# Norm statistics by block transposes, and their pieces put first and last in a step

## The chip, the cores and the metric

One core of a Trainium2 chip runs the whole kernel. The metric is the device time of one execution in microseconds (us), the median of three runs: 1723.39 (1720.31 to 1724.66) for the kernel before. TensorE multiplies matrices, VectorE works elementwise, ScalarE evaluates functions such as Sqrt and Silu, GpSimd (POOL) copies one partition's row to all partitions and issues some DMAs, SyncE (SP) issues the other DMAs. SBUF is the on-chip memory with 128 partitions, PSUM the memory that TensorE writes.

## What is computed

Four sequences of 1024 tokens with 1024 features pass four residual stages. Each stage ends in a norm over the features, without weights:

```python
x = L0_attn_data
x = _layernorm(x + _L0_attn_ref(x, ...), axis=-1)   # stage 0: product with a block-masked weight
x = _layernorm(x + _L0_ffn_ref(x, ...), axis=-1)    # stage 1: dense layer with a LoRA
x = _layernorm(x + _L1_attn_ref(x, ...), axis=-1)   # stage 2: a sequence model, below
x = _layernorm(x + _L1_ffn_ref(x, ...), axis=-1)    # stage 3: dense layer, LoRA mixed by a router
```

The sequence model projects to 128 features and runs four layers. Each layer does a norm, Silu, a long convolution (done here as a scan), a second norm and a small MLP with 512 hidden features; behind the last layer comes one more norm, and a projection back to 1024 features. All is float32.

## The kernel before, in words

In stages 0, 1 and 2 the activations lie with features on partitions and tokens along the free axis, in groups of 512 tokens (eight groups, g = 0 to 7; a sequence b is two groups). The big products of stages 0, 1 and 3 are done by seven half-size products in place of eight (Winograd's form of Strassen), so VectorE forms sums of operands ahead (`right_sums`, `left_sums`) and adds each product to its outputs (`z<-mm,z`) behind.

The mean is taken out of the weights beforehand, so a norm needs only the mean of the squares over the features, which are partitions. `rstd_rows` (L233) does this for 512 tokens. Four small products with the constant matrix `avg` (32 columns of 1/D) each take 128 tokens and write 32 equal rows, so that the PSUM tile `ps` of 128x128 holds the four quarters of the tokens in four groups of 32 equal rows. ScalarE takes the root of the whole tile into `sd` (L243), VectorE takes the reciprocal of the whole tile (L244), and `spread` (L247) has GpSimd copy one row out of each group of 32 to all 128 partitions, four broadcasts of 128 tokens. The result, `rs` or `crs`, is then multiplied into the activations. `ps` is one of two halves of a single PSUM tile, `stats`, one for the dense stages ("sd") and one for the sequence model ("sc"); other small products use the same tile.

There are 96 such norms. In 24 of them (`norm_rows`, L391) the squares come from stages 0, 1 and 2's end, summed in `ssum`. The other 72 belong to `sequence` (L846): four sequences, two halves j of 512 tokens each, and for each half two norms per layer and one at the end (`rows`, L861).

The order of the work is written out by hand. A clock counts steps. A step is one half-size product of eight matmuls on TensorE with its evictions, and then `tick()` runs the pieces that `plan` holds for that step, in the order in which they were put there. VectorE and TensorE execute strictly in program order (`InOrder`, L83). `put(at, piece, pe, dve)` puts a piece into a step and counts its cost; `put_in` (L336) spreads pieces over a range of steps by the room that the counted costs leave. Steps 0 to 223 belong to stages 0 and 1 (28 for each group g, 14 for each stage); steps 224 to 335 to stage 3. The sequence model of batch b runs beside them, from step 56b + 59. In `sequence` a norm's `rows` is at step `base` and at `base + 8` (7 for the last batch), and what uses it comes in the very next step: `first` (L879) or `normed` (L875), or `final` (L934) behind the last layer. `forward` (L910), the MLP, follows a step after `normed`; its first product a_ps reads `crs`. `later_rows` (L356) puts a dense norm into the next step from a given one that has no norm yet (`taken`).

Other names that matter: `merge` with its pieces `four` (L782) multiplies the LoRA factors of 16 rows into a weight, four weights a piece, with eight products in all for two pieces that fall in one step; `centre` (L1637) has ScalarE take away a mean and then GpSimd issue the store of the weight to DRAM; `wout_prep` (L1422) uses `stats` in step 59.

Of the kernel before, what the change touches and what calls it, by code (L numbers as in the profile page):

```python
# [10 lines left out]
F32 = mybir.dt.float32  # L11
# [42 lines left out]
def block_kernel(  # L54
# [175 lines left out]

        centre_by(w, centre_total(w), n)

    def rstd_rows(sums, n, avg, tag):  # L233

        seg = n // 4
        ps = stat(tag, S // 4)
        for j in range(4):
            T.matmul(
                ps[ds(32 * j, 32), :seg], lhsT=avg, rhs=sums[:, ds(j * seg, seg)],
                start=True, stop=True, tile_position=(0, 32 * j),  # L240
            )
        sd = small.tile([P, S // 4], F32, name="sd", tag=tag, bufs=1)
        A.activation(sd[:, :seg], ps[:, :seg], AF.Sqrt, bias=eps)  # L243
        V.reciprocal(sd[:, :seg], sd[:, :seg])  # L244
        return sd, seg

    def spread(dst, sd, seg):  # L247
        for j in range(4):
            G.partition_broadcast(  # L249
                dst[:, ds(j * seg, seg)], sd[32 * j : 32 * j + 1, :seg], channels=P  # L250
            )

# [98 lines left out]

    taken = set()

    def later_rows(n, piece):  # L356

        while clock[0] + n in taken:
            n += 1
        taken.add(clock[0] + n)  # L360
        later(n, piece)

    todo = {}

# [7 lines left out]
            adds.pop(0)()  # L372

    def tick():
        for piece in plan.pop(clock[0], ()):
            piece()
        clock[0] += 1


# [8 lines left out]
            A.activation(sq.rearrange("p (t n) -> p t n", n=HU), z, AF.Square, **kw)  # L388
            adds.append(lambda: V.tensor_tensor(ssum, ssum, sq, ALU.add))

    def norm_rows(ssum):  # L391
        rs = big("rs", [P, U], "rs", 2)
        sd, seg = rstd_rows(ssum, U, avg_d, "sd")
        spread(rs, sd, seg)
        return rs

    def z_tiles():
        return [k8("z1", [P, 2, 4, HU]) for _ in range(2)]
# [95 lines left out]
    def stage0(ops):  # L494
        ssum, z, t = big("ssum", [P, U], "ssum", 2), z_tiles(), t_tiles([4, HU])
        norm = {}

        def after(p, j):
            for c in range(2 * p, 2 * p + 2):
                square_in(z[j][:, :, c, :], None, ssum, p == 0 and j == 0 and c == 0)  # L500

        def early(p, i):
            cs = ds(2 * p, 2)
            lo, hi = ([z[j][:, h, cs, :] for h in range(2)] for j in range(2))
            for k in {4: (3,), 5: (1, 2), 6: (4,)}.get(i, ()):
                right_sum(k, lo, hi, t_out(t, cs))

        project(streamed(a0q_s), ops, z, after, early)
        later_rows(1, lambda: norm.update(rs=norm_rows(ssum)))
        return mixed(z, t), norm  # L510

    def finish_ln(at, name, z, ssum, bias, then):

        st = {}

        def rows():
            st["rs"] = norm_rows(ssum)

        def part(j):
            for c in range(2 * j, 2 * j + 2):  # L520
                rs = st["rs"]
                r = rs if len(z[c].shape) == 2 else rs.rearrange("p (t n) -> p t n", n=HU)
                V.scalar_tensor_tensor(z[c], z[c], bias[:, c : c + 1], r, ALU.add, ALU.mult)
            then(j)

        later_rows(at, rows)
        for j in range(4):
            todo[name, j] = partial(part, j)

# [316 lines left out]
    def sequence(b, at, layer, ahead):  # L846


        st = {}

        def h_of(j):
            return hs[b][:, ds(j * HF, HF)]

        def t_tile(name):
            return big(name, [P, HF], "t", 4)

        def square(j):
            st[j, "sq"] = sq = t_tile("csq")
            A.activation(sq, h_of(j), AF.Square)

        def rows(j):  # L861
            sd, seg = rstd_rows(st[j, "sq"], HF, avg_c, "sc")
            st[j, "y"] = rs = t_tile("crs")
            spread(rs, sd, seg)

        def tables_in(l, j):
            for k, (name, src) in enumerate((("ct", ct_s), ("sn", sn_s))):
                st[j, k] = t = big(name, [P, HF], name, 2)
                nc.sync.dma_start(t, src[l][:, ds(j * HF, HF)])

        def weights_in(l):
            st["mw"] = big("mw", [P, 2 * DFF], "mw", 1)
            nc.sync.dma_start(st["mw"], mw_s[l])

        def normed(j):  # L875
            y = st[j, "y"]
            V.tensor_tensor(y, h_of(j), y, ALU.mult)

        def first(l, j):  # L879
            normed(j)  # L880
            y = st[j, "y"]
            A.activation(y, y, AF.Silu, bias=col("ln1_b", l), scale=col("ln1_w", l))

        def scan(l, j, k):

            y = st[j, "y"]
            out = y if k else t_tile("u")
            V.tensor_tensor(out, st[j, k], y, ALU.mult)
            start = (g1i, g2i)[k][:, l : l + 1] if j == 0 else st["end", k]
            V.tensor_tensor_scan(  # L890
                out, rad[:, l : l + 1].to_broadcast([P, HF]), out, start, ALU.mult, ALU.add
            )
            if j == 0:
                st["end", k] = end = small.tile([P, 1], F32, name="end", tag=f"end{k}")
                A.copy(end, out[:, HF - 1 : HF])
            st[j, "out", k] = out

        def joined(j):
            u, y = st[j, "out", 0], st[j, "out", 1]
            V.tensor_tensor(u, st[j, 0], u, ALU.mult)  # L900
            V.tensor_tensor(y, st[j, 1], y, ALU.mult)
            V.tensor_tensor(u, u, y, ALU.add)

        def convolved(l, j):
            cv = spot("cv")
            T.matmul(cv, lhsT=csc[:, l, :], rhs=st[j, "out", 0], start=True, stop=True)
            V.tensor_tensor(h_of(j), h_of(j), cv, ALU.add)
            square(j)

        def forward(l, j, step):  # L910

            if step == 0:
                st["o"] = accp.tile([P, HF], F32, name="o2", tag="o2")
            for f in range(2 * step - 2, 2 * step):
                if f >= 0:
                    T.matmul(
                        st["o"], lhsT=st["mw"][:, ds(DFF + f * DIM, DIM)], rhs=st[f, "a"],
                        start=(f == 0), stop=(f == FC - 1),
                    )
            for f in range(2 * step, 2 * step + 2):  # L920
                if f < FC:
                    a = spot("a_ps")
                    T.matmul(
                        a, lhsT=st["mw"][:, ds(f * P, P)], rhs=st[j, "y"],
                        start=True, stop=True,
                    )
                    st[f, "a"] = s = big("a_sb", [P, HF], "a_sb", 4)
                    A.activation(s, a, AF.Silu, bias=b1c[:, l * FC + f : l * FC + f + 1])  # L928
            if step == 2:
                h = h_of(j)  # L930
                V.scalar_tensor_tensor(h, st["o"], b2c[:, l : l + 1], h, ALU.add, ALU.add)
                square(j)

        def final(j):  # L934
            V.tensor_tensor(h_of(j), h_of(j), st[j, "y"], ALU.mult)

        def put_rows(k, j):
            put(k, partial(rows, j), 0.9, 0.95)
            taken.add(k)

        slack = layer > SHORT
        for j in range(2):
            put(at + ahead * j - 1, partial(square, j))
        for l in range(DEPTH):
            for j in range(2):
                base = at + layer * l + ahead * j
                put(base - 2, partial(tables_in, l, j))
                put_rows(base, j)
                if j == 0:
                    put(base + ahead, partial(weights_in, l))  # L950
                put(base + 1, partial(first, l, j), 0.0, 0.7)
                put(base + 2, partial(scan, l, j, 0), 0.0, 1.9)
                put(base + 3, partial(scan, l, j, 1), 0.0, 1.9)
                put(base + 4, partial(joined, j), 0.0, 2.1)
                put(base + 5 + slack, partial(convolved, l, j), 0.9, 0.7)
                put_rows(base + 7 + slack, j)
                put(base + 8 + slack, partial(normed, j), 0.0, 0.7)
                put(base + 9 + slack, partial(forward, l, j, 0), 1.8, 0.0)
                put(base + 10 + slack, partial(forward, l, j, 1), 3.5, 0.0)
                put(base + 11 + slack, partial(forward, l, j, 2), 1.8, 0.75)  # L960
        for j in range(2):
            base = at + layer * DEPTH + ahead * j
            put_rows(base, j)
            put(base + 1, partial(final, j), 0.0, 0.7)


# [372 lines left out]
    right_sums(quarter[0], quarter[1], t_out(t1))  # L1339
    clock[0] = 14  # L1340
    norm1 = {}
    later(1, lambda: norm1.update(rs=norm_rows(ssum0)))

    def columns():
        tot = stat("sd", KC)
# [397 lines left out]
```

## Time and profile before

| | |
|---|---|
| median of three runs | 1723.39 us (1720.31 to 1724.66) |
| the profiled execution | 1722.86 us |
| its span, first to last instruction | 1721.1 us |
| mean granted TensorE clock | 0.992 |
| busy: TensorE, VectorE, ScalarE, GpSimd | 98%, 75%, 36%, 13% |
| mean DMA rate | 230 GB/s |

A span is what the profile covers; the execution's own time is 1.8 us longer here. Busy is the time in which an engine has an instruction in flight. A group's line on the page reads: line of the code (L104 is the helper that records all VectorE and TensorE instructions), engine, operation, output<-inputs, shapes, count, then busy us, mean ns of one, and the idle time of the engine just before these instructions with what ended it. On TensorE every float32 matmul shows as two records, so 16 records are the eight matmuls of a step. In the lists in order of time the columns are the start in us, the us that the entry takes, then engine, line, operation and names, and in brackets the idle time ahead and what ended it.

### The profile page before, as it was taken

What the parts mean: (1) busy time and instruction counts of PE and PEld (TensorE: products, weight loads), DVE (VectorE), ACT (ScalarE), POOL (GpSimd) and SP (SyncE); (2) the same over time, 40 slices, a digit from 0 to 9 for tenths busy, and PEclk for the clock granted to TensorE, in tenths of its full rate; (3) what the DMA queues carried; (4) which work ended last, traced back from release to release, by engine and by line L of the source; (5) the groups of instructions that cost most, each with busy time, mean ns of one, the idle gap of its engine ahead of it and who ended that gap; (6) DMA issues with size and microseconds to landing.
All of it is one profiled execution on the core that took longest, in us unless ns stands there. A gap on an engine that the chain in (4) does not pass through costs nothing.

```text
span 1721.1 us, 19210 instructions
## 1 busy us (share of the span) xinstructions
PE 1689.9 (98%) x6345; PEld 1047.8 (61%) x6345; DVE 1285.1 (75%) x2172; ACT 626.3 (36%) x1079; POOL 220.8 (13%) x454
## 2 busy tenths in 40 slices
PE   7999999999999999999999999999999999999998
PEld 3488887767676567666766676765444444444444
DVE  5799898677567779767886787677778878676743
ACT  4411112356333145443332454423344652333011
POOL 1110110211112012101120111011201200100000
PEclk9999999999999899999999999999999999999999
DMA  9968779856645885586978557786526737964211
GB/s 372 368 220 280 273 256 386 325 201 235 236 142 202 288 280 171 159 294 202 312 271 315 189 179 241 260 277 224 196 98 203 236 123 244 361 214 147 88 71 61
DMA packets 194709, 395.90 MB, mean 230 GB/s; under 512 B 16657, under 2 KB 105889, under 8 KB 189874
## 3 DMA queue, kind: packets, MB, share of 16 engines
q1 hardware_dynamic: 187602, 371.82, 63.0%
q0 software_dynamic: 6048, 21.37, 3.3%
q10 hardware_dynamic: 960, 1.48, 0.2%
q8 instruction: 50, 0.82, 0.2%
q14 instruction: 49, 0.40, 0.1%
HBM read 268.39 MB, written 126.23 MB: 229 GB/s over the span
## 4 chain that ended last, share of the span: by engine, by line
PE 71%; DVE 6%; DMA 1%; ACT 1%; issue 1%; SPq 0%; POOL 0%; ACTq 0%; DVEq 0%
PE mm L104 57%; PE a_ps L104 6%; PE o L104 5%; DVE z L104 2%; PE stats L104 2%; PE cv L104 1%; DMA w<-a_s 1%; DVE x L104 1%; DVE u L104 1%; DVE crs L104 1%; DVE w L104 1%; DVE tt L104 1%; DVE s L104 0%; DVE sd L104 0%; DVE ssum L104 0%
## 5 line engine op out<-in xcount | busy, mean ns | idle before, releaser
L104 DVE TENSOR_TENSOR z<-mm,z 128x512 f32<-128x512 f32 x339 | 226.5, 683 | 256.3 <-PE mm L104 255.1
L104 PE MATMUL mm<-tt,wq 128*128 128x256 f32 x1792 | 407.5, 381 | 0.0
L104 PEld LDWEIGHTS mm<-tt,wq 128*128 128x128 f32 x1792 | 337.4, 190 | 75.2 <-issue 22.7
L249 POOL PARTITION_BROADCAST crs<-sd x288 | 140.6, 597 | 844.6 <-DVE sd L104 652.7
L104 PE MATMUL mm<-w3q,x 128*128 128x512 f32 x384 | 173.0, 596 | 0.0
L104 PE MATMUL mm<-xT,wq 128*128 128x256 f32 x672 | 154.8, 385 | 0.0
L104 PE MATMUL mm<-z,wq 128*128 128x256 f32 x672 | 152.0, 380 | 0.0
L104 PEld LDWEIGHTS mm<-z,wq 128*128 128x128 f32 x672 | 127.2, 190 | 29.3 <-issue 9.4
L104 PEld LDWEIGHTS mm<-xT,wq 128*128 128x128 f32 x672 | 127.3, 192 | 26.3 <-issue 5.8
L104 PE MATMUL mm<-w3q,s 128*128 128x512 f32 x288 | 130.4, 596 | 0.0
L104 PE MATMUL a_ps<-crs,mw 128*128 128x512 f32 x256 | 121.1, 595 | 6.2 <-DVE crs L104 6.2
L104 PEld LDWEIGHTS mm<-w3q,x 128*128 128x128 f32 x384 | 71.9, 190 | 88.2 <-issue 87.5
L104 DVE TENSOR_TENSOR ssum<-ssum,sq 128x512 f32<-128x512 f32 x168 | 115.4, 688 | 11.7 <-ACT sq L388 5.1
L928 ACT ACTIVATE a_sb<-a_ps,b1c 128x512 f32<-128x512 f32 x128 | 86.2, 683 | 104.3 <-PE a_ps L104 103.9
L104 DVE RECIPROCAL sd<-sd 128x128 f32<-128x128 f32 x96 | 91.1, 949 | 41.6 <-ACT sd L243 40.3
L104 PE MATMUL o<-a_sb,mw 128*128 128x512 f32 x256 | 120.6, 593 | 0.4 <-ACT a_sb L928 0.4
L104 PE MATMUL mm<-b,aT 16*128 16x512 f32 (+1 forms) x256 | 94.9, 638 | 5.4 <-DVE z L104 4.8
L688 ACT ACTIVATE sq<-z 128x512 f32<-128x512 f32 (+1 forms) x65 | 40.4, 622 | 157.0 <-DVE z L104 143.8
L104 PEld LDWEIGHTS mm<-w3q,s 128*128 128x128 f32 x288 | 53.8, 190 | 65.4 <-issue 64.5
L104 DVE TENSOR_TENSOR w<-w,mm 128x512 f32<-128x512 f32 x128 | 81.6, 678 | 13.5 <-PE mm L104 10.4
L243 ACT ACTIVATE sd<-stats,eps 128x128 f32<-128x128 f32 x96 | 35.1, 366 | 139.3 <-PE stats L104 105.0
L104 PEld LDWEIGHTS a_ps<-crs,mw 128*128 128x128 f32 x256 | 48.0, 190 | 60.2 <-issue 49.7
(248 smaller groups left out, 2142.5 us busy)
## 6 DMA issues: line engine op xcount, KB each, us to landing
wq<-a0q_s SPq DMA_DIRECT2D x98, 512.0 KB, 4.4
wq<-a1q_s SPq DMA_DIRECT2D x98, 512.0 KB, 4.5
w<-a_s SPq DMA_DIRECT2D x48, 512.0 KB, 6.2
w3q<-a3q_s SPq DMA_DIRECT2D x21, 1024.0 KB, 8.1
a1q_s<-w SPq DMA_DIRECT2D x64, 256.0 KB, 2.4
x_s<-z SPq DMA_DIRECT2D x16, 1024.0 KB, 5.2
x<-x_s SPq DMA_DIRECT2D x64, 256.0 KB, 5.7
x_s<-x SPq DMA_DIRECT2D x128, 128.0 KB, 2.4
```

The source lines that it names most:

```text
L104: ins = op(*args, **kw)
L243: A.activation(sd[:, :seg], ps[:, :seg], AF.Sqrt, bias=eps)
L249: G.partition_broadcast(dst[:, ds(j * seg, seg)], sd[32 * j : 32 * j + 1, :seg], channels=P)
L688: A.activation(sq[:, cols], z[:, m, ds(n * HF, HF)][:, cols], AF.Square, accum_out=st[:, m, n : n + 1] if out is None else out,)
L928: A.activation(s, a, AF.Silu, bias=b1c[:, l * FC + f : l * FC + f + 1])
```

## The change

`rstd_rows` becomes two functions. `small_sums` does the four small products as before; then VectorE turns the 128x128 tile by blocks of 32x32, after which each group of 32 columns has equal columns, and ScalarE takes the root of one column of each group only, four columns in all. `rows_of_roots` takes the reciprocal of these four columns on VectorE, and then VectorE turns them back, reading each of the four columns 32 times, so that `sd` has the layout that `spread` needs. The four broadcasts are the same.

A norm is now two pieces. `tick` runs three lists: `firsts`, which holds the sums of the step's norms, then `plan`, then `lasts`, which holds the reciprocal, the turn back and the broadcasts. A norm keeps its step. The planner counts 0.5 and 0.5 for a norm in place of 0.9 and 0.95; the dense ones are counted too when they are put.

```diff
-    def rstd_rows(sums, n, avg, tag):
-
-        seg = n // 4
-        ps = stat(tag, S // 4)
+    def small_sums(sums, avg, tag):
+
+
+        ps = stat(tag, P)
         for j in range(4):
             T.matmul(
-                ps[ds(32 * j, 32), :seg], lhsT=avg, rhs=sums[:, ds(j * seg, seg)],
+                ps[ds(32 * j, 32), :], lhsT=avg, rhs=sums[:, ds(j * P, P)],
                 start=True, stop=True, tile_position=(0, 32 * j),
             )
-        sd = small.tile([P, S // 4], F32, name="sd", tag=tag, bufs=1)
-        A.activation(sd[:, :seg], ps[:, :seg], AF.Sqrt, bias=eps)
-        V.reciprocal(sd[:, :seg], sd[:, :seg])
-        return sd, seg
...
+        t = small.tile([P, P], F32, name="across", tag="across" + tag, bufs=1)
+        V.transpose(t, ps)
+        r = small.tile([P, 4], F32, name="root", tag="root" + tag, bufs=1)
+        A.activation(r, t.rearrange("p (b q) -> p b q", q=32)[:, :, 0], AF.Sqrt, bias=eps)
+        return r
+
+    def rows_of_roots(r, tag):
+
+        V.reciprocal(r, r)
+        sd = small.tile([P, P], F32, name="sd", tag=tag, bufs=1)
+        V.transpose(
+            sd.rearrange("p (b q) -> p b q", q=32),
+            r.rearrange("p (b o) -> p b o", o=1).to_broadcast([P, 4, 32]),
+        )
+        return sd
...
-    def later_rows(n, piece):
-
+    firsts, lasts = {}, {}
+
+    def put_rows(at, sums, rest):
+
+        taken.add(at)
+        firsts.setdefault(at, []).append(sums)
+        lasts.setdefault(at, []).append(rest)
+        count(at, 0.5, 0.5)
+
+    def later_rows(n, sums, rest):
         while clock[0] + n in taken:
             n += 1
-        taken.add(clock[0] + n)
-        later(n, piece)
+        put_rows(clock[0] + n, sums, rest)
...
     def tick():
-        for piece in plan.pop(clock[0], ()):
-            piece()
+        for pieces in (firsts, plan, lasts):
+            for piece in pieces.pop(clock[0], ()):
+                piece()
         clock[0] += 1
...
         def rows(j):
-            sd, seg = rstd_rows(st[j, "sq"], HF, avg_c, "sc")
+            st[j, "root"] = small_sums(st[j, "sq"], avg_c, "sc")
+
+        def rest(j):
             st[j, "y"] = rs = t_tile("crs")
-            spread(rs, sd, seg)
+            spread(rs, rows_of_roots(st[j, "root"], "sc"))
...
-        def put_rows(k, j):
-            put(k, partial(rows, j), 0.9, 0.95)
-            taken.add(k)
...
-                put_rows(base, j)
+                put_rows(base, partial(rows, j), partial(rest, j))
```

`norm_rows` becomes `dense_rows(n, ssum, then)`, which splits in the same way: `small_sums` in the first list; `spread` and what takes the result in the last.

## The prediction

> **What bounds the kernel now.** I read the page first, then TensorE's waits, its busy time in stretches of 20 us, and around each stretch that was short the instructions in order of time. On the page:
>
> ```profile
> PE 1689.9 (98%) x6345; PEld 1047.8 (61%) x6345; DVE 1285.1 (75%) x2172; ACT 626.3 (36%) x1079; POOL 220.8 (13%) x454
> ...
> L104 DVE RECIPROCAL sd<-sd 128x128 f32<-128x128 f32 x96 | 91.1, 949 | 41.6 <-ACT sd L243 40.3
> ...
> L243 ACT ACTIVATE sd<-stats,eps 128x128 f32<-128x128 f32 x96 | 35.1, 366 | 139.3 <-PE stats L104 105.0
> ```
>
> TensorE is busy 1689.9 of 1721.1 us, so every stall together is 31.2 us. The edit touches 96 norms; their reciprocal holds VectorE 91.1 us, plus 41.6 us in which VectorE waited for ScalarE's root. But VectorE is only 75% busy: its time counts only where TensorE waits for it. TensorE's waits:
>
> ```profile
> PE stats L104 <- DVE rows L104: 9.8, 2, 7.2
> PE a_ps L104 <- DVE crs L104: 6.2, 5, 3.1
> PE mm L104 <- DVE z L104: 4.8, 2, 2.4
> ```
>
> The first is the start of the kernel (masks), which the edit doesn't touch. The others are the target. By stretch (columns: stretch, its us, then busy us of PE, PEld, DVE, ACT, POOL; last three clock, DMA share, GB/s):
>
> ```profile
> 340.00:360.00 20.00, 16.51 (x64) 11.65 (x63) 15.70 (x23) 13.57 (x21) 4.64 (x6) 1.00 0.49 169
> ...
> 560.00:580.00 20.00, 17.58 (x82) 12.40 (x80) 19.32 (x29) 5.55 (x10) 3.39 (x4) 0.98 0.94 316
> 580.00:600.00 20.00, 20.00 (x50) 10.38 (x49) 9.03 (x16) 2.55 (x4) 0.00 (x0) 0.77 0.74 261
> ...
> 720.00:740.00 20.00, 18.73 (x70) 13.00 (x69) 19.79 (x29) 10.96 (x24) 2.67 (x4) 1.00 0.84 269
> ...
> 900.00:920.00 20.00, 17.06 (x45) 7.82 (x44) 12.92 (x20) 1.01 (x3) 2.67 (x3) 0.83 0.89 308
> ```
>
> The first 20 us lose 11.4 (8.60 busy) and everything from 1700 us 6.2 (14.85 busy). That leaves about 13.6 us of stall in the middle, nearly all in five places: A, at 348.93 us (3.06, a_ps waits for crs); B, at 578.96 (2.42, a product waits for a bank that VectorE frees); D, B's twin one batch later (2.42 + 0.52 at 905.98 and 907.77); C and E, at 725.73 and 1051.38 (1.27 each, a_ps waits for crs). After B and D the clock is 0.77 and 0.83 for 20 us: another 4.6 and 3.4 us. So the most that faster norms could give is about 20 us, and only if those places empty.
>
> **What one norm costs.** Out: one reciprocal of 949 ns, one root of 366. In, on VectorE: a transpose from PSUM, a reciprocal of four columns, a transpose with a broadcast input. A 128x1 reciprocal takes 147 ns, so a column costs (949-147)/127 = 6.3 and four cost 166. No transpose is in the trace. The nearest row, TENSOR_SCALAR 128x128, is 280 ns. So 0.28+0.17+0.28 = 0.73 us in place of 0.95: 0.22 off, 21 us over 96. Here a rule speaks against the edit: the Trainium skill, "VectorE: DVE Perf Modes", Rules for kernel authors, says to minimize the number of chained VectorE operations, since each pays its own flush; by its transposes (The three transpose paths, 311 ns, bf16; no f32 figure) a norm costs 0.31+0.17+0.31 = 0.79, still 0.16 off (15 us in all). I take the row. If f32 took two passes, 0.56 each, a norm would cost 1.29, 0.34 more than now; that is the upper end. A gain above 0.5 is excluded, as neither transpose can be under the 147 ns of the smallest VectorE rows.
>
> ScalarE's root shrinks, but now waits for VectorE's transpose; what stands behind it is the Silu of `forward` and the squares. Only steps 115, 171, 227 and 244 have both a norm and a Silu that TensorE needs. In 115 the transpose can start at 548.9, root to 549.4, table load 1.28, two Silus to 552.1; `o` starts at 552.85. Covered by 0.7 us, so nothing; without that cover 0.7 each.
>
> TensorE's four small products are the same ones, only first in the step. In every step their sums were ready before the step's product ended (the tightest, csq at 744.22, has 0.06 us and nothing ahead of it): nothing.
>
> The planner's costs change (0.9, 0.95 to 0.5, 0.5). I worked `put_in` through with both: no piece changes step. Only the order inside steps changes.
>
> **What moves.** The four broadcasts now start behind the whole step's VectorE work, and are used by `normed`, `first` or `final` in the next step. This is the new wait: VectorE stands there, with its evictions queued behind. I went through all 72 norms of the sequence from the rows. Where the next step's eviction waits for TensorE anyway, the shift is within 0.1 us; up to +0.9 appears where VectorE is behind, mostly with a_ps 1.3 to 2.5 us from being late. The places that count:
>
> A. The reciprocal stood 1.96 us waiting for the root, then:
>
> ```profile
> 342.14 0.95 DVE L104 RECIPROCAL sd<-sd 128x128 f32<-128x128 f32 x1 [1.96 <-ACT sd L243]
> ...
> 348.19 0.68 DVE L104 TENSOR_TENSOR crs<-h,crs 128x512 f32<-128x512 f32 x1
> ```
>
> The transpose goes at 340.15, then scan, tt, w (3.45 us) to 343.9, the rest to 344.35, eviction and multiplication to 346.1; broadcasts from 344.5, done at 345.8 to 346.9. So crs starts 1.2 to 2.1 earlier: -1.6 (the stall of 3.06 covers it). A 0.28 us stall at 310.61 goes likewise: -0.3.
>
> B and D. The norm is in the stretch in which VectorE is behind:
>
> ```profile
> 571.12 0.95 DVE L104 RECIPROCAL sd<-sd 128x128 f32<-128x128 f32 x1
> 571.98 0.63 DVE L104 TENSOR_TENSOR crs<-sn,crs 128x512 f32<-128x512 f32 x1
> 572.65 1.28 DVE L104 TENSOR_TENSOR_SCAN crs<-rad,g2i,crs 128x512 f32<-128x512 f32 x1
> 573.85 1.51 DVE L104 TENSOR_TENSOR ssum<-ssum,sq 128x512 f32<-128x512 f32 x2
> 575.68 0.69 DVE L104 TENSOR_TENSOR h<-h,crs 128x512 f32<-128x512 f32 x1 [0.32 <-POOL crs L249]
> ...
> 578.22 0.68 DVE L104 TENSOR_TENSOR z<-mm,z 128x512 f32<-128x512 f32 x1
> ```
>
> New: transpose to 571.37, scan to 573.24, rest to 573.72, broadcasts 0.17 later. How long do they take? Beside scan and adds 3.39; beside two adds alone 2.00:
>
> ```profile
> 572.26 3.39 POOL L249 PARTITION_BROADCAST crs<-sd  x4 [16.91 <-DVE sd L104]
> ```
>
> ```profile
> 534.80 2.00 POOL L249 PARTITION_BROADCAST crs<-sd  x4 [25.82 <-PE mm L104]
> ```
>
> and 1.26 where VectorE idles or reads PSUM (540.20). The Trainium skill, "GPSIMD Engine Reference", 1. Specifications, says GpSimd's SBUF interfaces are shared with VectorE, contended by instructions with two SBUF inputs. Taken as full blocking, two adds would make it 1.26+1.5 = 2.8, and `final` would start 1.0 late; the row has 2.00, thus 573.72+0.17+2.00+0.03 = 575.92, 0.24 late. I take the row: +0.24 in each, +0.5; ends -0.5 (1.26) and +1.6 (3.39) each.
>
> C and E. From 717.03 VectorE runs without a gap to crs at 724.99. New: the rest ends at 723.45, eviction and tt reach 724.75, broadcasts end 724.9 to 725.55. Shift -0.1 to +0.6; +0.3 each, +0.6.
>
> Small ones. Steps 213 and 218, a_ps 0.05 and 0.41 from being late, shifts +0.2 and +0.9 (less 0.57 that VectorE arrives earlier): +0.3. GpSimd's queue: in step 80 the broadcasts pass behind the store of `centre`, which waits for ScalarE's w (376.10 to 377.25), then 0.55 to issue: broadcasts end near 379.1 instead of 376.81; a_ps at 379.29 slips to 379.9: +0.6. Step 85 is moved so too, with VectorE slack: nothing. At 259.63 wout's products wait for the reader of `stats`, which is now the transpose behind two evictions (260.03 + 0.28): +0.7.
>
> Sum: -1.6 - 0.3 + 0.5 + 0.6 + 0.3 + 0.6 + 0.7 = +0.8 us. The profiled execution took 1722.86 us (span 1721.1 and 1.8 around it), 0.5 under the median 1723.39; so 1723.7 on it, 1724.2 on the median.
>
> **Rivals.** Gain: B and D lose enough stall that the clock isn't lowered after them. For: 3.06 us of stall at A left the clock at 1.00, so the dips hang on little (16-row products, then a gap). Against: VectorE there saves only 0.22. Price: 4.6+3.4 = 8.0, with A -1.9 and the other terms at their low ends about 0: 1723.4-9.9, about 1713.5. Chance 0.13.
>
> Slower: the wait for the broadcasts takes the place of the wait for the root. If four broadcasts take 3.4 wherever VectorE has work, B and D start 1.6 late (3.3), C and E 2.0 (4.0), 213 and 218 1.9 each (3.8), step 80 2.7, 259.63 0.7, and A keeps only 0.3, with 0.3 at 310.61: +13.9, 1737. It decides from about 2.4 us a group, where B, D, C and E together pass 3 us; 2.4 to 3.4 spans 1729 to 1737. For: 3.3 to 3.5 is seen four times in the first 720 us. Against: those all lie beside scans, which are now ahead of them. Chance 0.21.
>
> The edit doesn't do what it says: f32 transposes take 0.56, VectorE's norms grow by 0.34 each: B to E and the two small steps +0.5 each, 1727. Chance 0.06.
>
> **The numbers.** Likeliest 1724.2 (chance 0.60; own range 1719 to 1728.5). About 0.3% (5 us) is what a measurement here can tell from no change. Faster takes the first rival: 0.13. Slower takes the second and a little of the likeliest's tail: 0.23. The rest, 0.64, is within. 1716 to 1731 leaves out about one in ten at either end.
>
> **What would show it.** Reciprocal rows of 128x4 near 166 ns and transposes near 280; VectorE busy some 20 us lower (1265); the 40 us wait for the root gone; a new wait of VectorE for POOL crs, some 5 to 20 us instead of 5.6; A's stall near 1.5; B and D still there, 0.77 and 0.83 after them; TensorE busy unchanged. I am wrong if a transpose takes over 0.5, if TensorE waits for the small sums, or if groups of four broadcasts take over 2.4 in steps 118, 143, 174 and 199.

## The result, and the profile after

The changed kernel takes 1738.74 us in the median of six runs (1737.18 to 1742.46), the kernel before 1723.31 on the same chip (1720.31 to 1725.01, six runs): a ratio of 1.0092, 95% interval 1.0078 to 1.0105, so some 15 us slower. The prediction was 1724.2 with a range of 1716 to 1731: wrong. The profiled execution took 1738.17 us, span 1736.5.

The page after: its busy line, the broadcasts and the root, and from the list of groups the transposes and the reciprocal.

```profile
PE 1695.4 (98%) x6345; PEld 1049.3 (60%) x6345; DVE 1261.2 (73%) x2364; ACT 621.8 (36%) x1079; POOL 172.7 (10%) x454
...
L260 POOL PARTITION_BROADCAST crs<-sd x288 | 99.8, 456 | 914.3 <-DVE sd L104 834.2
```

```profile
L104 DVE STREAM_TRANSPOSE sd<-root 128x128 f32<-128x128 f32 x96 | 29.9, 312 | 3.3
L104 DVE STREAM_TRANSPOSE across<-stats 128x128 f32<-128x128 f32 x96 | 29.5, 307 | 3.1 <-PE stats L104 3.0
...
L104 DVE RECIPROCAL root<-root 128x4 f32<-128x4 f32 x96 | 16.4, 171 | 18.4 <-ACT root L245 18.2
```

The arithmetic is what was promised: a norm holds VectorE for 0.79 us by its three instructions (0.95 before), and VectorE is busy 24 us less. The four broadcasts of a group overlap, so that the 72 groups of the sequence model take 99.8/72 = 1.4 us each, where they took 140.6/72 = 1.95. Yet TensorE waits more, and in other places (columns: us in total, times, longest):

```profile
PE a_ps L104 <- DVE crs L104: 10.9, 5, 6.1
...
PE mm L104 <- DVE z L104: 5.9, 2, 3.0
PE o L104 <- ACT a_sb L953: 2.1, 3, 0.8
PE stats L104 <- DVE across L104: 2.0, 2, 1.2
PE mm L104 <- ACT z L1328: 1.5, 1, 1.5
```

The longest, 6.1 us at a_ps, is new. In the list by stretches (columns as in the prediction) it stands out in 840 to 860 us (the kernel before: busy all 20 us, clock 1.00); 60 to 80 us is short too (19.93 us and 0.91 before). The stretches from 580 and 920 us lie behind B and D:

```profile
60.00:80.00 20.00, 18.45 (x45) 6.47 (x38) 17.28 (x32) 8.29 (x15) 2.79 (x4) 0.83 0.99 363
...
580.00:600.00 20.00, 18.62 (x41) 9.25 (x42) 9.52 (x16) 1.32 (x2) 0.00 (x0) 0.74 0.74 251
...
840.00:860.00 20.00, 13.86 (x40) 8.57 (x39) 11.11 (x15) 2.07 (x3) 1.34 (x4) 0.83 0.79 274
...
920.00:940.00 20.00, 20.00 (x50) 10.68 (x50) 8.99 (x15) 2.68 (x4) 0.00 (x0) 0.77 0.76 244
```

The 15.3 us between the two profiled executions can be added up. TensorE's waits of over 0.3 us were 23.7 us together and are 34.1: +10.4. The lower clock, summed as (1 - clock) x 20 us over all whole stretches of 20 us, cost 12.4 us and costs 17.2: +4.8. Together 15.2. By place: the stop near 848 us with its dip is 6.1 + 3.4 = 9.5; the first 80 us have 2.1 of new stops and 1.6 more of dip (3.4 in place of 1.8).

What happened near 848 us is on GpSimd's list after:

```profile
836.11 1.11 POOL L798 DMA_INDIRECT aT<-lo_s,pick  x1 [2.75 <-issue]
837.53 1.49 POOL L798 DMA_INDIRECT b<-lo_s,pick  x1 [0.31 <-issue]
839.93 0.42 POOL L260 PARTITION_BROADCAST crs<-sd  x1 [0.92 <-DVE sd L104]
846.59 0.99 POOL L260 PARTITION_BROADCAST crs<-sd  x3 [6.24 <-DMA b<-lo_s,pick]
```

The norm is the one of step 162. Its first broadcast goes at once; the other three wait 6.24 us for a DMA to land that has nothing to do with them. The two DMAs belong to step 164 (`merge`'s `start` for the last batch, L792). In the kernel before, the four broadcasts went first:

```profile
832.50 1.50 POOL L249 PARTITION_BROADCAST crs<-sd  x4 [2.65 <-DVE sd L104]
834.27 1.39 POOL L775 DMA_INDIRECT aT<-lo_s,pick  x1 [0.27 <-POOL crs L249]
835.96 1.53 POOL L775 DMA_INDIRECT b<-lo_s,pick  x1 [0.31 <-issue]
```

After the change VectorE stands in order behind crs, TensorE behind VectorE:

```profile
847.61 0.69 DVE L104 TENSOR_TENSOR crs<-h,crs 128x512 f32<-128x512 f32 x1 [7.28 <-POOL crs L260]
```

```profile
848.36 3.78 PE L104 MATMUL a_ps<-crs,mw 128*128 128x512 f32 x4 [6.14 <-DVE crs L104]
```

The code fixes the order of VectorE and TensorE (`InOrder`), not GpSimd's: the framework's scheduler places its instructions. With the broadcasts moved to the end of step 162 it put the DMAs of step 164 first. The built kernel also has the second broadcast behind these DMAs wait until both have landed (842.99 and 846.44 us). In the kernel before the same two waits are there, but fall on the group at 861.80 us, when both have long landed (842.37 and 846.36).

### The profile page after: what moved, and what is told of

It is laid out like the page before. It is cut to its first block, busy times and chain, and to the rows that moved or that the text cites. A ratio compares the mean times of both kernels' runs of the same rounds, so it can differ in the third digit from the quotient of the medians.

```text
span 1736.5 us, 19324 instructions
## 1 busy us (share of the span) xinstructions
PE 1695.4 (98%) x6345; PEld 1049.3 (60%) x6345; DVE 1261.2 (73%) x2364; ACT 621.8 (36%) x1079; POOL 172.7 (10%) x454
## 4 chain that ended last, share of the span: by engine, by line
PE 86%; DVE 7%; DMA 3%; ACT 2%; issue 1%; POOL 1%; ACTq 0%; DVEq 0%; SPq 0%; POOLq 0%
PE mm L104 71%; PE a_ps L104 6%; PE o L104 6%; PE stats L104 2%; PE cv L104 2%; DVE z L104 2%; DVE w L104 1%; DVE s L104 1%; POOL crs L260 1%; DVE u L104 1%; DVE crs L104 1%; DVE x L104 1%; DMA w<-a_s 1%; DMA b<-lo_s,pick 1%; DVE ssum L104 0%
## 5 line engine op out<-in xcount | busy, mean ns | idle before, releaser
L260 POOL PARTITION_BROADCAST crs<-sd x288 | 99.8, 456 | 914.3 <-DVE sd L104 834.2
L245 ACT ACTIVATE root<-across,eps 128x4 f32<-128x4 f32 x96 | 28.9, 301 | 174.7 <-DVE across L104 165.4
L104 PEld LDWEIGHTS o<-a_sb,mw 128*128 128x128 f32 x256 | 47.9, 190 | 45.2 <-issue 37.3
```

What stands on the lines that cost most here:

```text
L104: ins = op(*args, **kw)
L245: A.activation(r, t.rearrange("p (b q) -> p b q", q=32)[:, :, 0], AF.Sqrt, bias=eps)
L260: G.partition_broadcast(dst[:, ds(j * P, P)], sd[32 * j : 32 * j + 1, :], channels=P)
```

## The experiments

The theories: 1, GpSimd's order near 848 us is the cause; 2, the later place of the broadcasts in all norms is; 3, the arithmetic is. A fourth, the place of the tiles in memory, came up with the first runs.

**The DMAs put back behind the broadcasts.**

```diff
+            newest["b"] = G.partition_broadcast(...)       # in spread
...
+                    if clock[0] > 150:                     # in merge's start
+                        tc.add_manual_dep(ins.ins, newest["b"].ins.name, ...)
```

> The changed kernel with one more dependence: batch 3's two indirect DMAs (aT<-lo_s,pick and b<-lo_s,pick, step 164) are put behind the last broadcast issued before them, those of step 162's norm, on GpSimd's queue, as they stood in the kernel before. Nothing else differs. Theory 1 (three of the four broadcasts of step 162 wait for the landing of a DMA that the scheduler put ahead of them, 6.2 us, then VectorE 7.3, TensorE 6.1 and a clock dip): the eviction times of the changed kernel fall behind those before by 8.5 us between steps 163 and 166, so this takes back 7 to 9 us: 1730 to 1732; the wait of 6.1 us of a_ps at 848 us is gone and TensorE is busy for over 19 us in the stretch 840 to 860. Theory 2 (the later place of the broadcasts in all 72 norms costs the time, 15.4 us spread evenly, and the 848 us stop is only where it shows): at most 1 to 2 us back, 1736 to 1738. If the two DMAs, now landing some 6 us later, stop VectorE at its scaling of b, part of the gain is gone: 1733 to 1735.

Measured: 1729.39 us (1726.43 to 1732.24), 9.3 less than the changed kernel, or 8.2 when each is taken against the kernel before that was timed beside it; against before 1.0044 (1.0031 to 1.0057). GpSimd's list now:

```profile
838.38 1.26 POOL L262 PARTITION_BROADCAST crs<-sd  x4 [6.35 <-DVE sd L104]
839.91 1.43 POOL L802 DMA_INDIRECT aT<-lo_s,pick  x1 [0.27 <-POOL crs L262]
841.65 1.46 POOL L802 DMA_INDIRECT b<-lo_s,pick  x1 [0.31 <-issue]
```

The stop of 6.1 us and its dip, 9.5 us by the profile, are gone (the profiled execution is the fastest of the five). VectorE now waits 4.23 us for b at 850.73, and TensorE stops 0.92 us at 859.01. Theory 1 holds for 8 to 9 of the 15 us; 6 to 7 are left.

**One half of the change at a time.** First the new arithmetic as one piece at the old place in each step, with the same dependence:

```diff
-        firsts.setdefault(at, []).append(sums)
-        lasts.setdefault(at, []).append(rest)
+        put(at, both, 0.5, 0.5)        # both: sums(), then rest()
```

> The new arithmetic alone: sums, root, reciprocal and both transposes and the broadcasts as one piece at the old place in each step, with batch 3's indirect DMAs behind the broadcasts of step 162 as before. Theory 1 (GpSimd's order is the cause and the arithmetic is nearly free): 1721 to 1726, no stop of over 3 us of TensorE between 830 and 860 us. Theory 3 (the chain with two transposes and a small root is the cause, since each norm crosses VectorE three times where it crossed once, and VectorE stands in order behind each crossing): 1733 to 1740. Theory 2 (later place): 1722 to 1725, since nothing is moved later.

Measured: 1731.37 us (1727.03 to 1733.70), 1.0047 (1.0034 to 1.0060). No theory had this: the arithmetic is not nearly free. Alone it costs 9.2 us, where both halves together, without the stop, cost 7.2.

Then the new order with the old arithmetic: the root of the whole tile in the first list, the whole reciprocal and the broadcasts in the last.

```diff
-        V.transpose(t, ps)
-        A.activation(r, t.rearrange(...)[:, :, 0], AF.Sqrt, bias=eps)
+        A.activation(sd, ps, AF.Sqrt, bias=eps)
...
         V.reciprocal(r, r)             # of the whole 128x128 tile
-        V.transpose(sd.rearrange(...), r.rearrange(...).to_broadcast([P, 4, 32]))
```

> The new order alone: the sums and the root of the whole 128x128 tile first in each step, the whole reciprocal and the four broadcasts last, arithmetic as before. GpSimd's order of step 162 is the changed kernel's: batch 3's two indirect DMAs ahead of that step's broadcasts. Theory 1: 8 to 10 us slower than before for that stop alone, 1732 to 1736, and the stop of a_ps of about 6 us near 848 us is there. Theory 2: 1736 to 1740, spread over the norms. Theory 3 (arithmetic): 1722 to 1726.

Measured: 1736.65 us (1734.24 to 1739.43), 1.0084 (1.0071 to 1.0097), with the stop at a_ps (5.78 us at 845.73). The time is just over what theory 1 had (1732 to 1736) and inside theory 2's range, so the next run has to decide: the same with the DMAs behind the broadcasts:

> As the run with the new order alone, with batch 3's two indirect DMAs behind the broadcasts of step 162. Theory 1: 1723 to 1728, 7 to 9 us faster than the new order alone, and no stop of over 3 us at a_ps near 848 us. Theory 2 (later place of all broadcasts): within 2 us of the new order alone, 1734 to 1738. Theory 3: 1722 to 1726.

Measured: 1729.39 us (1728.69 to 1733.13), 1.0046 (1.0033 to 1.0059). That is 7.3 less, so theory 1 is seen a second time, with other arithmetic, and theory 2's forecast (within 2 us of the run before) fails. The level is 1.4 above what theory 1 had, 7.2 over the kernel before, so the new order costs something besides. TensorE's waits of over 0.3 us are 27.5 us here (23.7 before); the rest of the 7.2 is not accounted for.

**The place of the tiles.** With TensorE's instructions matched one by one, the three kernels with the new arithmetic are 3.1 to 3.7 us behind the kernel before at 100 us, the two with the old arithmetic in the new order 0.8 and 0.9. The order of the DMAs there is the same. But the new small tiles push all large tiles by 64 bytes in each partition: they begin at byte 27,968, not 27,904. So the kernel before was run with 64 unused bytes:

```diff
+    small.tile([P, 16], F32, name="pad", bufs=1)
```

> The kernel before with one unused tile of 64 bytes a partition ahead of the large tiles, so that these lie where the changed kernel has them (from byte 27,968 of a partition instead of 27,904); nothing else differs. The three kernels with the new arithmetic all lose 3 to 4 us in the first 100 us, with the same order of DMAs as before and 373 to 377 GB/s between 10 and 20 us where the kernel before had 394; the two with the old arithmetic lose 0.1. Theory 4 (the two tiles that the change adds push the large tiles by 64 bytes, and DMAs into and out of them are slower there): 1724 to 1727, 2 to 4 us slower than before, about 376 GB/s between 10 and 20 us, and the DMA b<-lo_s,pick lands some 3 us later (VectorE's scaling of b at about 59 us, not 55.7). If the place of the tiles is nothing: 1721 to 1723.5.

Measured: 1726.45 us (1722.29 to 1730.53), 1.0025 (1.0013 to 1.0036): slower by 4 us in the median, and nothing in the code but the addresses differs. (The profile is of the fastest of its seven runs, 1722.29 us, so it shows the start of the kernel and not the 4 us.) The stretch from 20 to 30 us (last column GB/s) of the kernel before, and of this one:

```profile
20.00:30.00 10.00, 10.00 (x29) 4.80 (x28) 5.64 (x11) 5.05 (x7) 0.00 (x0) 1.00 1.05 400
```

```profile
20.00:30.00 10.00, 10.00 (x29) 4.83 (x28) 5.67 (x11) 5.02 (x7) 0.00 (x0) 1.00 1.05 380
```

The DMA engines are just as busy (1.05) and move 5% less. VectorE's scaling of b comes at 56.98 us, not 55.72, and TensorE has a new stop of 1.10 us at 64.08 with a clock of 0.83 behind it. Three more distances:

> The kernel before with 128 unused bytes a partition ahead of the large tiles (from byte 28,032: a multiple of 128, not of 256). If what slows the DMAs of the first 60 us is a place that is an odd multiple of 64 bytes (as the 64 bytes of the changed kernel and of the shifted kernel before give): as before, about 400 GB/s between 20 and 30 us and 1721 to 1724. If it is any place other than 256 modulo 512: about 380 GB/s and 1724 to 1728.

Measured: 381 GB/s, 1725.74 us (20 runs), 1.0014 (1.0007 to 1.0021).

> The kernel before with 192 unused bytes ahead of the large tiles (from byte 28,096: an odd multiple of 64). Odd multiples of 64 slow the DMAs: about 380 GB/s between 20 and 30 us, 1724 to 1728. If only the very place of the changed kernel (64 bytes on) is slow: 400 GB/s and 1721 to 1724.

Measured: 380 GB/s, 1725.86 us (15 runs), 1.0014 (1.0006 to 1.0022).

> The kernel before with 256 unused bytes a partition ahead of the large tiles (from byte 28,160, a multiple of 512; the kernel before has 256 modulo 512, and 64, 128 and 192 bytes more all gave 380 GB/s between 20 and 30 us). If multiples of 256 are the good places: about 400 GB/s there, 1722 to 1724. If only the old place is: about 380 GB/s, 1725 to 1727. If a multiple of 512 is better than 256 modulo 512: over 410 GB/s and under 1722.

Measured: 404 GB/s, 1723.39 us (13 runs), 1.0000 (0.9991 to 1.0008). So 0 and 256 bytes more are fast, 64, 128 and 192 slow: tiles at multiples of 256 bytes. All 14 profiles agree: 400 to 404 GB/s in the eight with the large tiles at such a place, 379 to 381 in the six without. The Trainium skill, "DMA: Bandwidth & Descriptors", How a descriptor splits into AXI transactions, says that a descriptor that does not start at a multiple of 256 bytes has its first transaction begin at the boundary below, with bytes fetched for nothing. The boundary agrees. Its count of wasted bytes grows with the distance (64 against 192); the rates here are the same for all three. The runs show the boundary, not its cause.

Then the changed kernel with the DMAs put right and 448 unused bytes, which puts its large tiles on a multiple of 256 again:

> The changed kernel with batch 3's two indirect DMAs behind the broadcasts of step 162 and an unused tile of 448 bytes, which puts the large tiles at the same place modulo 512 bytes as before (256, where the changed kernel has 320). Theory 4: 1725 to 1727, 2.5 to 4 us faster than with the DMAs alone put right (1729.4), and no offset of over 1 us against the kernel before in the first 100 us; what is left, some 4 us, is the new order's own (VectorE's longer stops at the four places where TensorE waits for it). If place is nothing: 1728 to 1731.

Measured: 1726.75 us (1725.60 to 1730.93, ten runs), 1.0029 (1.0020 to 1.0039): 2.6 less than without the unused bytes, inside its range, and no new stop near 65 us. The other sign did not come: less than 1 us behind at 100 us was expected, and the profiled execution (1729.03, itself slower than the median) is 2.0 behind, with the scaling of b at 57.04. The two intervals overlap, so this pair alone would not show the gain; the shifts of the kernel before do. And the arithmetic alone, placed so:

> The new arithmetic alone at the old place in each step, batch 3's DMAs behind the broadcasts of step 162, and the large tiles at the place modulo 512 that they have before (448 unused bytes): the arithmetic without the other two causes. TensorE's two long stops for a bank (mm<-DVE z) stay at 4.3 us each where the kernel before has 2.4, and the first 100 us are as before. That is 4 us of stops more, 2 less at 349 us, 2 more at 417: 1725 to 1729. If the arithmetic cost nothing once the tiles are placed: 1722 to 1724.

Measured: 1731.04 us (1727.87 to 1732.76), 1.0043 (1.0030 to 1.0057); 2 above the upper end of its range, and placing gave 0.3 here. Its DMAs run at 400 GB/s between 20 and 30 us, but b still came late (57.90; 57.50 in the fast run with 256 bytes) and TensorE stopped 0.89 us at 65.00, so in a single profile a late b does not tell a bad place. With six and five runs this run and the one not placed leave -4 to +2 us open, so this pair neither supports the placing nor speaks against it. The two stops for a bank were 4.35 us each, as expected.

**Why the arithmetic costs.** Around B, VectorE and then ScalarE in the run of the arithmetic alone, placed:

```profile
576.35 0.31 DVE L104 STREAM_TRANSPOSE across<-stats 128x128 f32<-128x128 f32 x1
578.74 0.18 DVE L104 RECIPROCAL root<-root 128x4 f32<-128x4 f32 x1 [2.08 <-ACT root L246]
```

```profile
576.47 0.63 ACT L413 ACTIVATE sq<-z 128x512 f32<-128x512 f32 x1 [0.70 <-DVE ssum L104]
577.11 1.28 ACT L246 ACT_TABLE_LOAD   x1
578.41 0.30 ACT L246 ACTIVATE root<-across,eps 128x4 f32<-128x4 f32 x1
```

In the kernel before, the root needed TensorE alone: ScalarE loaded its table at 567.00 and had the root done by 568.7, 2.4 us before VectorE came for it at 571.12:

```profile
568.30 0.37 ACT L243 ACTIVATE sd<-stats,eps 128x128 f32<-128x128 f32 x1
```

Now the root needs VectorE's transpose first, and VectorE needs the root: a square of `z` and the table load lie in between. Over the kernel VectorE waits 97.6 us for the root in this run, 40.3 before. In the whole change the plan's pieces between the two halves cover most of that (18.2 us); there the wait moves to the broadcasts. The changed kernel with the DMAs put right and placed, around B:

```profile
577.41 0.18 DVE L104 RECIPROCAL root<-root 128x4 f32<-128x4 f32 x1 [0.19 <-ACT root L246]
...
577.86 1.38 DVE L104 TENSOR_TENSOR ssum<-ssum,sq 128x512 f32<-128x512 f32 x2
580.11 0.69 DVE L104 TENSOR_TENSOR h<-h,crs 128x512 f32<-128x512 f32 x1 [0.88 <-POOL crs L263]
```

From the first `ssum` to `z<-mm,z` VectorE takes 574.42 to 582.65 = 8.23 us, before 570.52 to 578.22 = 7.70: 0.53 more, and TensorE's stop is 2.94, before 2.42. Of the 0.53, 0.56 is the longer wait for the broadcasts (0.88 in place of 0.32) and 0.19 that for the root; the shorter arithmetic gives some 0.2 back.

**No VectorE in the root.** One ScalarE instruction for root and reciprocal, in the kernel before, takes VectorE out of the chain. It also takes the reciprocal's 0.95 us off VectorE, so it does not tell the two apart.

```diff
-        A.activation(sd[:, :seg], ps[:, :seg], AF.Sqrt, bias=eps)
-        V.reciprocal(sd[:, :seg], sd[:, :seg])
+        A.activation(sd[:, :seg], ps[:, :seg], AF.Abs_reciprocal_sqrt, bias=eps)
```

> The kernel before with one ScalarE instruction for the root and the reciprocal (Abs_reciprocal_sqrt from PSUM, 128x128) in place of Sqrt on ScalarE and RECIPROCAL on VectorE; order and place of the tiles as before. VectorE loses 72 instructions of 0.95 us, and no longer stands in its queue for the root. If VectorE's crossing with ScalarE is what the stops of TensorE at 348.9, 579.0, 725.7, 906.0 and 1051.4 us hang on (3.1, 2.4, 1.3, 2.4, 1.3 us), each becomes shorter by about 1 us: 1715 to 1720. If they hang on something else: 1721 to 1724. A table load of ScalarE more in each norm (1.28 us) would give part of it back.

Measured: 1716.33 us (1715.39 to 1719.24), 0.9968 (0.9955 to 0.9980). (There are 96 such instructions, not the 72 written there.) TensorE's waits:

```profile
PE mm L104 <- DVE z L104: 2.7, 2, 1.3
...
PE a_ps L104 <- DVE crs L104: 1.0, 2, 0.5
```

A has no stop left, B and D 1.3 us (2.4), C and E 0.5 (1.3). At B the reciprocal did not wait for the root before (571.12 in the prediction's lines), so the 1.1 us gained there are about the reciprocal's own 0.95; at A the reciprocal also waited 1.96 for the root. A new stop of 1.31 us, small products that wait for VectorE's tile `r`, came at 1562.37. The instruction takes 367 ns, as the root did, with 119 table loads in the kernel in place of 107. With this root, and sums and broadcasts both ahead of the step's other pieces:

> As the run with one instruction for root and reciprocal, with the sums, root and broadcasts of each norm moved ahead of the other pieces of the step. TensorE's sums then ask for squares that may just be made, and the broadcasts come earlier than in any other version, so that no VectorE instruction waits for them. If early broadcasts help: 1713 to 1718. If TensorE's wait for ScalarE's squares grows (0.9 to 1.5 us once in the runs with the new order): 1718 to 1722. GpSimd has batch 3's DMAs behind the broadcasts of step 162 in it as in the kernel before.

Measured: 1716.29 us (1714.73 to 1718.28), 0.9962 (0.9950 to 0.9974). The same: with VectorE out of the chain, putting the norm first in the step is worth nothing that can be measured. Both versions beat both kernels.

The design without the 848 us stop, each median less that of the kernel before timed beside it (about 0.1% or 2 us is open in each):

| | arithmetic before | arithmetic new |
|---|---|---|
| order before | 0 | +8.1 (placed), +9.2 (not placed) |
| order new | +7.2 | +4.2 (placed), +7.2 (not placed) |

The two halves do not add up: each alone costs more than both together. For the new arithmetic the reason is seen above, since the new order covers its wait for the root. Why the new order costs 7.2 with the old arithmetic stays open beyond the waits named there.

## Why the prediction was wrong

Of the 15.4 us, 8.2 to 9.3 are GpSimd's order (changed kernel less the run with the DMAs behind), 2.6 to 3.0 the place of the tiles (that run less the placed one), and 3.4 to 4.2 the norms themselves, against the +0.8 predicted for everything. In each pair one figure is from the plain medians, the other from medians against the kernel before timed beside them.

- **The step that failed: "Only the order inside steps changes", and with it the one line on GpSimd's queue.** It took GpSimd's order to follow the code and asked only which store of the same step the broadcasts pass (step 80). GpSimd's order is the scheduler's, and the broadcasts of step 162 were passed by two DMAs of step 164. What the first should have asked of every queue is which instruction without a fixed order can come ahead, and how long the next one then waits: here for a landing, 6.24 us on GpSimd, 6.14 on TensorE and a clock of 0.83 behind it.
- **Left out: the addresses.** No term for the 64 bytes by which the new small tiles move the large ones; +2.8 to +4 us by the runs of the kernel before at 64, 128 and 192 bytes.
- **VectorE's time:** 1265 predicted, 1261 measured; 166 ns for the small reciprocal, 171 measured (the trace before had reciprocals of 128x4 at 172 and 178). The transposes were put at 280 ns by the nearest row; they take 307 and 312. Here the 311 of the Trainium skill ("VectorE: DVE Perf Modes", The three transpose paths), set aside for the row, was right, though it stands for bf16. It is 6 us of VectorE over 96 norms, and little of that is on the path.
- **A:** -1.6 expected, the stop 3.06 to 0.96 (-2.1), but `o<-a_sb` behind it now stops 0.80 and 0.67 (0.43 before): -1.1 net. The 0.3 at 310.61 went, but a stop of 0.77 came at 305.82: there the sums wait for the transpose that reads `stats`. "TensorE's four small products: nothing" was wrong there by that much, and one of the signs named for being wrong, that TensorE waits for the small sums, is there.
- **B and D:** +0.24 each; measured +0.53 each (2.95). The broadcasts took 1.95 us, the row chosen had 2.00; the missing 0.3 is the wait for the root and the longer transpose. **C and E:** +0.3 each, measured +0.43 (1.70).
- **The small ones:** `wout`, +0.7 expected, +0.76 measured. Steps 213 and 218, +0.3 expected: the a_ps at 1142.01 stops 0.36 us, and what the prediction took for a margin of 0.05 was already a stop of 0.30 before (1127.49); the one at 1180.53 stops 0.1, none before. The Silu of step 227, "covered, 0.7 without cover": 0.66 at 1221.49, so the cover was gone. Step 80, +0.6: no stop there.
- **The rivals:** the slower one had the right size, 1737, for a wrong reason. Its deciding point was 2.4 us for a group of broadcasts; they take 1.4 on average and, but for the group that waited for the DMAs, 2.25 at most. Its wait, VectorE for the broadcasts, is there (27.9 us; 20.7 with the DMAs put right, at the top of the 5 to 20 expected), and the 7.3 us in it that matter came from the queue, not from the broadcasts' length. That its size was right is luck. The gain did not come: the stops at B and D grew, and the dips after them stayed (0.74, 0.77).

So the sum for the norms was short by B to E 0.8, A 0.5, the sums' wait at 305.82 0.8 and the Silu 0.7, less 0.6 for step 80 and 0.1 for steps 213 and 218: 2.1, which makes 2.9 of the predicted 0.8. Measured are 3.4 to 4.2; what is between is not resolved by these runs.

## What to carry to other kernels

When a piece is moved, list for each queue whose order is not fixed in the code what the builder may now put ahead of it, and fix the order where a slow DMA is among it; compare the built order of every engine before and after. When a change adds tiles, see whether the large ones still start where they did (here, at multiples of 256 bytes), and time the old kernel with the new addresses before blaming the new instructions. Between two engines that execute in order, one crossing more can cost more than shorter instructions give back: the new arithmetic alone took 0.16 us of VectorE's time off each norm and lost 8 us once placed. One instruction on ScalarE in place of root and reciprocal gained 6 us; these runs do not divide that between the crossing and the 0.95 us of VectorE's time that went with it.

## What the runs showed of the hardware

- Large tiles at a multiple of 256 bytes in a partition: 400 to 404 GB/s between 20 and 30 us in eight profiles; 64, 128 or 192 bytes beside it: 379 to 381 in six. The DMA engines were equally busy (a share of 1.05 or 1.06).
- The float32 transpose by 32x32 blocks of a 128x128 tile takes 307 ns from PSUM, and 312 ns with an input of four columns that is read 32 times each.
- A TensorE stop of 6.1 us was followed by a clock of 0.83 over the stretch 840 to 860; stops of 2.4 to 3.0 us at B and D by 0.74 to 0.85 in most runs, while 3.06 us at A in the kernel before left it at 1.00. With stops of 1.3 us at B and D, in the run with one root, the clock was still 0.94 behind B and 0.83 behind D. What decides it is not shown.
- Four broadcasts took 1.26 us at 838.38 (the changed kernel with the DMAs behind), 1.95 beside VectorE's two adds at 578.12, and 3.35 beside a scan and adds at 579.46 in the run of the arithmetic alone.
